# Cross-attention on one Trainium2 core: the first loads dealt between two issuing engines and turned head by head

## The chip, the cores and the metric

The kernel runs on one core of one Trainium2 chip. A core has TensorE (matmuls, into PSUM), VectorE (DVE in the profile), ScalarE (ACT), GpSimd (POOL) and SyncE (SP, which here only issues DMA transfers). Transfers are moved by 16 DMA engines. The metric is the device time of one execution in microseconds; lower is better. Everything is float32.

## The reference

Sixteen batches of 256 queries attend to 77 context rows with eight heads of 256. The output is projected, the input is added, and the sum is normalised.

```python
Q = (img_embed @ Wq).reshape(B, -1, H, D).transpose(0, 2, 1, 3)   # H = 8, D = 256
K = (sent_embed @ Wk).reshape(B, -1, H, D).transpose(0, 2, 1, 3)  # sent_embed: 16 x 77 x 192
V = (sent_embed @ Wv).reshape(B, -1, H, D).transpose(0, 2, 1, 3)
score = jnp.einsum('bhqd,bhkd->bhqk', Q, K) / math.sqrt(D)
attn = jax.nn.softmax(jnp.where(mask, score, -jnp.inf), axis=-1)
ctx = jnp.einsum('bhqk,bhkd->bqhd', attn, V).reshape(B, -1, H * D)
out = ctx @ Wo + img_embed
mu, var = jnp.mean(out, -1, keepdims=True), jnp.var(out, -1, keepdims=True)
return (out - mu) * jax.lax.rsqrt(var + EPS) * gamma + beta
```

## The kernel before

Instead of Q and K the kernel forms, for each head, G = Wk Wqᵀ / 16 (192 x 256). The product of the context with G, called a, meets the input x directly, so Q and K are never made. Wv and Wo are multiplied in the same way. G has 192 rows: the first 128 are kept in `gA` (one slice for each head), the last 64 in `gB` (two heads share one slice, one in each half of the partitions).

The order of the work is written by hand; each engine executes its instructions in the order of the program. The opening, which is all that the change touches, runs like this:

- SP issues the loads in the order of the code: `wk_nat` (Wk of heads 0, 1, first 128 rows, L623), `wq_nat` (Wq of heads 0, 1, one transfer each, L625), `wk_last` (the last 64 rows of Wk, L627), `c_sb` (the context of the first batches, L628). Then, for each pair of heads a = 1, 2, 3, four transfers of Wk and four of Wq (`load_blocks`, L598), each into 32 partitions, in blocks of 128 columns. Wv, Wo, the first input tiles, the mask and the rest of the context follow. In a `wq_blk` load a partition r takes the rows r, r + 32, r + 64 and so on of Wq.
- TensorE first runs six matmuls on zeros (`keep_busy(6)`, L664). Then it turns (transposes) the four blocks of `wk_nat` (`turn_k`), those of `wq_nat` (`turn_q`, once for each head), forms G of head 0 (`g_of`), turns `wk_last`, forms G of head 1, turns the context (`turn_c`, L714), forms the last rows of G (`rest_of_g`), and makes `a` of heads 0 and 1 (`a_of_pairs`, L181 and L193).
- For a = 1, 2, 3 the blocks are turned by DVE in squares of 32 x 32 (`turn_blk`, L703), Wk first, then Wq; TensorE makes the last 64 rows of G (`rest_of_g_of_pair`, matmul L819, tile `phb`), copied to `gB` by DVE (L828), then the first 128 (`g_of_pair`, matmul L803, tile `pgb`), copied to `gA` by ACT (L811), and then `a` of the pair.
- GpSimd makes the identity matrix for the turning, clears the unused columns of the two tiles `p_ring` (L99), and is next needed for the copy of the context's rows into `cB` (L725).

After this come the Wv and Wo products and the loop over batches (scores, softmax, product with V, normalisation), which the change leaves as it is.

Transfers and engines are joined by semaphores. The built program gives SP's transfers eight semaphores in turn; a transfer that takes a semaphore for the second time waits until the transfer that held it has landed.

Of the kernel before, what the change touches and what calls it, by code (L numbers as in the profile page):

```python
# [9 lines left out]
F32 = mybir.dt.float32  # L10
I32 = mybir.dt.int32
AF = mybir.ActivationFunctionType
ALU = mybir.AluOpType
# [3 lines left out]
P = 128  # L17
H = 8
D = 256
# [8 lines left out]
def kernel(  # L28
# [13 lines left out]
    nc = tc.nc  # L42
    B, S, DI = x.shape
    S2, DL = c.shape[1], c.shape[2]
# [6 lines left out]
    NF = H // 2  # L51
    KR = S2 - KM
    BK = 32
    NM = P // BK
# [16 lines left out]
    ps_mm = ctx.enter_context(tc.tile_pool(name="ps_mm", bufs=8, space=PSUM))  # L71
# [3 lines left out]
    ident = const.tile([P, P], F32, tag="ident", name="ident")  # L75
# [4 lines left out]
    gA = const.tile([P, H, DI], F32, tag="gA", name="gA")  # L80

    gB = const.tile([P, NF, DI], F32, tag="gB", name="gB")
# [12 lines left out]
    cRA = const.tile([P, B, KR], F32, tag="cRA", name="cRA")  # L95
    cRB = const.tile([P, B, KR], F32, tag="cRB", name="cRB")
    p_ring = [const.tile([P, NM, PW], F32, tag=f"p{i}", name=f"p_{i}") for i in range(2)]
    for p in p_ring:
        nc.gpsimd.memset(p[:, :, 2 * S2 :], 0.0)  # L99
    bias = const.tile([P, B, S2], F32, tag="bias", name="bias")  # L100
    bias_f = bias.rearrange("p b k -> p (b k)")
    bet = const.tile([P, DI], F32, tag="bet", name="bet")
# [4 lines left out]
    c_rows = c.rearrange("b k l -> (b k) l").rearrange("(r p) l -> p r l", p=CR)  # L107

    def flat(ap):
        return ap.rearrange("p a b -> p (a b)")  # L110

    def half(i):
        return slice(i * LB, (i + 1) * LB)
# [466 lines left out]
    with tc.tile_pool(name="wonce", bufs=1) as wp:  # L580
        first = -(-GB * S2 // CR)
        c_sb = wp.tile([CR, first, DL], F32, tag="c", name="c_sb")
# [3 lines left out]
        wk_nat = wp.tile([P, 2 * D], F32, tag="wk", name="wk_nat")  # L586
        wk_last = wp.tile([P, D], F32, tag="wl", name="wk_last")

        wq_blk = wp.tile([P, NF - 1, DI // BK, P], F32, tag="wqb", name="wq_blk")
        wk_blk = wp.tile([P, NF - 1, NL, P], F32, tag="wkb", name="wk_blk")  # L590
        wq_blocks = wq.rearrange("(m r) (a i f) -> a i r m f", r=BK, a=NF, i=NM)
        wk_blocks = wk.rearrange("(m r) (a i f) -> a i r m f", r=BK, a=NF, i=NM)
        wq_rows = wq[:, : 2 * D].rearrange("(t p) f -> p t f", p=P)
        wk_ends = wk[P:, : 2 * D].rearrange("r (e f) -> r e f", e=2)
# [25 lines left out]
            nc.gpsimd.tensor_copy(flat(cB)[:LB, rest], flat(cB)[LB:, rest])  # L620
            nc.gpsimd.tensor_copy(cRB, cB[:, :, KM:])

        nc.sync.dma_start(wk_nat, wk[:P, : 2 * D])  # L623
        for e in range(2):
            nc.sync.dma_start(wq_nat[:, :, e * D : (e + 1) * D], wq_rows[:, :, e * D : (e + 1) * D])  # L625
        for e in range(2):
            nc.sync.dma_start(wk_last[half(e)], wk_ends[:, e])  # L627
        nc.sync.dma_start(c_sb, c_rows[:, :first, :])  # L628
        for a in range(1, NF):
            load_blocks(wk_blk[:, a - 1], wk_blocks[a])  # L630
            load_blocks(wq_blk[:, a - 1], wq_blocks[a])
# [30 lines left out]
        def keep_busy(n):  # L662
            for i in range(n):
                nc.tensor.matmul(idle, gam[:, :P], gam[:, :P], start=True, stop=True)  # L664

        keep_busy(6)


        qT_03 = const.tile([P, 2, 4, DI], F32, tag="xg0", name="qT_03")
# [1 line left out]
        kT_03 = const.tile([P, 2, 4, DL], F32, tag="xg2", name="kT_03")  # L671
        kT_12 = const.tile([P, 2, 4, DL], F32, tag="xg3", name="kT_12")
        qT = qT_03[:, 0].rearrange("p (e dc) d -> p e dc d", e=2)
        kT = kT_03[:, 0].rearrange("p (e dc) l -> p e dc l", e=2)
# [3 lines left out]
        def turn_q(e):  # L678
            for dc, copy in enumerate((nc.vector.tensor_copy, nc.scalar.copy)):
                pt = ps_mm.tile([P, 2, P], F32, tag="mm", name=f"pt_q_{e}_{dc}")  # L680
                for t in range(2):
                    nc.tensor.transpose(
                        pt[:, t], wq_nat[:, t, e * D + dc * P : e * D + (dc + 1) * P], ident
                    )
                copy(qT[:, e, dc], flat(pt))

        def turn_k():
            pt = ps_mm.tile([P, 4, P], F32, tag="mm", name="pt_k")
            for n in range(4):
                nc.tensor.transpose(pt[:, n], wk_nat[:, n * P : (n + 1) * P], ident)  # L690
            nc.scalar.copy(kT_03[:, 0, :, :P], pt)

        def turn_k_last():
            pt = ps_mm.tile([P, 2, P], F32, tag="mm", name="pt_kl")
# [79 lines left out]
        def g_of(e):  # L774

            pg = ps_mm.tile([P, DI], F32, tag="mm", name=f"pg_{e}")
            for dc in range(2):
                nc.tensor.matmul(
                    pg, kT[:, e, dc, :P], qT[:, e, dc], start=(dc == 0), stop=(dc == 1)
                )  # L780
            nc.scalar.mul(gA[:, e], pg, D ** -0.5)

        def rest_of_g():
# [10 lines left out]
                    )  # L794
            nc.vector.tensor_scalar(gB[:, 0], ph, D ** -0.5, None, ALU.mult)

        def g_of_pair(a):

            banks = [ps_mm.tile([P, DI], F32, tag="mm", name=f"pgb_{a}_{e}") for e in range(2)]
            for n in range(4):  # L800
                for i in range(2):
                    for e in range(2):
                        nc.tensor.matmul(  # L803
                            banks[e][half(i)],
                            kT_blk[a][half(e), n, half(i)],
                            qT_blk[a][half(e), n],
                            start=(n == 0),
                            stop=(n == 3),
                        )
            for e, o in enumerate(banks):  # L810
                nc.scalar.mul(gA[:, 2 * a + e], o, D ** -0.5)  # L811

        def rest_of_g_of_pair(a):

            banks = [ps_mm.tile([P, P], F32, tag="mm", name=f"phb_{a}_{e}") for e in range(2)]
            for n in range(4):
                for i in range(2):
                    for e in range(2):
                        nc.tensor.matmul(  # L819
                            banks[e][half(i)],  # L820
                            kT_blk[a][half(e), n, P:],
                            qT_blk[a][half(e), n, i * P : (i + 1) * P],
                            start=(n == 0),
                            stop=(n == 3),
                        )
            for e, o in enumerate(banks):
                for i in range(2):
                    nc.vector.tensor_scalar(  # L828
                        gB[half(e), a, i * P : (i + 1) * P], o[half(i)], D ** -0.5, None, ALU.mult
                    )  # L830

        def a_of_pairs(*pairs, rest_first=False):
            part_A, part_B, copies = prepare_a(0, pairs, rest_first=rest_first)
# [2 lines left out]
            for dst, src in copies():  # L836
                nc.scalar.copy(dst, src)

        turn_k()
        turn_q(0)  # L840
        turn_q(1)
        g_of(0)
        turn_k_last()
        g_of(1)
# [4 lines left out]
        for a in range(1, NF):  # L849
            rest_of_g_of_pair(a)  # L850
            g_of_pair(a)
            if a < NF - 1:
                turn_blk(a + 1)
            else:
                for i in range(3):
                    turn_v(i)
            a_of_pairs(a, rest_first=True)
# [84 lines left out]
    for b in range(-1, B - 1):  # L942
# [16 lines left out]
        g, n = (b + 1) // GB + 1, (b + 1) % GB  # L959
# [126 lines left out]
```

## Time and profile before

| What | us |
|---|---|
| median of three runs (lowest to highest) | 272.66 (272.11 to 273.08) |
| the profiled execution: time | 271.64 |
| the profiled execution: span, first to last instruction | 269.8 |
| TensorE busy | 263.8 |
| DVE busy | 185.9 |
| GpSimd busy | 171.3 |
| ACT busy | 156.5 |
| first turning of Wk on TensorE starts | 4.05 |
| context, issue to landing | 4.5 |
| wq_blk loads, issue to landing (shortest, median, longest) | 4.2, 4.8, 5.0 |

Times in the profile count from the start of the span. A row of the timeline gives start, length, engine, line, operation, output and inputs, the number of instructions, and in brackets the idle time before it with what ended it. "PEld" is TensorE's loading of weights, "SPq" the queue of SP. The chain that ended last is followed back from the last instruction, at each step to what released it or to the instruction before it. A row of the windows gives the stretch and its length, busy time and number of instructions of PE, PEld, DVE, ACT and POOL, then the granted TensorE clock, the busy share of the DMA engines and GB/s.

### The profile page before, as it was taken

To read this page: it belongs to the slowest core of one execution; us is meant where nothing else is said; L and a number is where in the kernel's file an instruction comes from. 1 tells how busy PE (TensorE), PEld (TensorE's weight loads), DVE (VectorE), ACT (ScalarE), POOL (GpSimd) and SP (SyncE) were. 2 spreads that over 40 slices of the span, in tenths; PEclk is the share of its full clock that TensorE was granted. 3 is DMA by queue.
4 is the path that set the end of the run, shared out by engine and by line. 5 is a ranking of instruction groups with operands and counts; after the bars stand their busy time and mean duration, and the time that the engine had idled before them with its cause. 6 is when DMAs were issued, how large, how long until landed. Compare 5 with 4: busy or idle time off the path is not lost.

```text
span 269.8 us, 14465 instructions
## 1 busy us (share of the span) xinstructions
PE 263.8 (98%) x6152; PEld 190.7 (71%) x6152; DVE 185.9 (69%) x809; ACT 156.5 (58%) x652; POOL 171.3 (63%) x231
## 2 busy tenths in 40 slices
PE   8999999999999999999999999999999999999993
PEld 7555578854994599459954995499769969684662
DVE  1454958583564858864796379646977898988765
ACT  3244335635858555964587377728685592945752
POOL 1000005716399757995699759964999798966654
PEclk9999999999999999999999999999999999999999
DMA  6998999988000010361027100910091010110102
GB/s 196 200 198 183 305 188 154 280 147 155 5 4 4 2 45 5 97 104 41 5 62 139 44 4 15 187 41 6 5 195 46 5 43 6 41 44 2 62 22 79
DMA packets 42512, 22.69 MB, mean 84 GB/s; under 512 B 23680, under 2 KB 41680, under 8 KB 42448
## 3 DMA queue, kind: packets, MB, share of 16 engines
q1 hardware_dynamic: 42448, 21.77, 36.4%
q8 instruction: 48, 0.79, 1.2%
q14 instruction: 16, 0.13, 0.1%
HBM read 17.57 MB, written 4.19 MB: 81 GB/s over the span
## 4 chain that ended last, share of the span: by engine, by line
PE 91%; DVE 4%; DMA 3%; SPq 1%; issue 0%; DVEq 0%
PE ps L291 23%; PE pa L181 12%; PE pv L215 11%; PE po L436 10%; PE pm L436 9%; PE pa L193 6%; PE pv L226 6%; PE po L369 4%; PE pu L742 3%; PE pgb L803 2%; DMA wq_blk<-in_L_xattn_Wq_dram 2%; DMA c_sb<-in_ctx_dram 2%; PE pr L251 1%; PE pw L756 1%; PE phb L819 1%; PE pr L262 1%
## 5 line engine op out<-in xcount | busy, mean ns | idle before, releaser
L326 ACT ACTIVATE e<-s,top 128x77 f32<-128x77 f32 x256 | 83.8, 346 | 45.5 <-DVE top L308 38.5
L291 PE MATMUL ps<-a,xT 128*32 128x154 f32 x2048 | 69.9, 294 | 0.0
L291 PEld LDWEIGHTS ps<-a,xT 128*32 128x32 f32 x2048 | 66.2, 110 | 1.2 <-issue 0.4
L347 POOL TENSOR_TENSOR p<-e,rden 128x512 f32<-128x512 f32 x64 | 47.7, 771 | 23.3 <-DVE rden L341 23.3
L308 DVE CUSTOM_DVE_ANT_0 s<-ps,bias 128x77 f32<-128x77 f32 x256 | 43.6, 232 | 15.4 <-PE ps L291 15.3
L326 ACT ACTIVATION_READ_ACCUMULATOR e<-s,top 128x1 f32 x208 | 39.0, 187 | 0.0
L181 PE MATMUL pa<-cA,gA 128*32 128x308 f32 (+1 forms) x576 | 36.6, 394 | 0.0
L471 POOL TENSOR_TENSOR xg<-xg,m 128x256 f32<-128x256 f32 x39 | 28.7, 737 | 7.8 <-DVE xg L485 5.8
L181 PEld LDWEIGHTS pa<-cA,gA 128*32 128x32 f32 x576 | 18.3, 110 | 21.1 <-issue 6.7
L215 PE MATMUL pv<-uA,cA 128*32 128x512 f32 x256 | 30.6, 595 | 0.0
L554 DVE SCALAR_TENSOR_TENSOR xg<-xg,rstd,bet 128x256 f32<-128x256 f32 x26 | 21.2, 816 | 12.9 <-ACT rstd L515 11.5
L400 POOL TENSOR_TENSOR ts<-vw 128x768 f32<-128x768 f32 x13 | 24.0, 1847 | 7.6 <-ACT vw L928 7.6
L357 DVE STREAM_TRANSPOSE pT<-p 128x640 f32<-128x640 f32 x32 | 25.7, 822 | 3.2 <-POOL p L347 3.1
L928 ACT COPY vw<-pv 128x512 f32<-128x512 f32 x32 | 17.7, 584 | 14.7 <-PE pv L215 7.7
L485 DVE TENSOR_TENSOR xg<-po,xg 128x256 f32<-128x256 f32 x31 | 11.6, 407 | 13.4 <-PE po L436 12.4
L308 DVE DVE_READ_ACCUMULATOR2_ANT top<- 128x1 f32 x256 | 20.8, 81 | 0.0
L574 POOL TENSOR_TENSOR nan<-nan 128x4 f32<-128x4 f32 (+1 forms) x2 | 0.4, 209 | 31.8 <-DVE nan L573 31.8
L193 PE MATMUL pa<-cB,gB 64*32 64x308 f32 (+1 forms) x576 | 20.6, 392 | 0.0
L928 ACT COPY a<-pa 128x308 f32<-128x308 f32 (+1 forms) x56 | 18.9, 399 | 1.7 <-PE pa L181 0.2
L193 PEld LDWEIGHTS pa<-cB,gB 64*32 64x32 f32 x576 | 10.6, 106 | 12.2 <-issue 7.7
L226 PE MATMUL pv<-uB,cB 64*32 64x512 f32 x256 | 17.3, 597 | 0.0
L535 DVE SCALAR_TENSOR_TENSOR xg<-xg,mv,gam 128x256 f32<-128x256 f32 x27 | 16.7, 619 | 0.1
(119 smaller groups left out, 412.1 us busy)
## 6 DMA issues: line engine op xcount, KB each, us to landing
xT<-in_x_dram SPq DMA_DIRECT2D x32, 128.0 KB, 5.9
xg<-in_x_dram SPq DMA_DIRECT2D x6, 512.0 KB, 5.2
out_dram<-xg SPq DMA_DIRECT2D x11, 256.0 KB, 2.3
wo<-in_L_xattn_Wo_dram SPq DMA_DIRECT2D x4, 512.0 KB, 5.3
wq_blk<-in_L_xattn_Wq_dram SPq DMA_DIRECT2D x12, 128.0 KB, 4.8
wvT<-in_L_xattn_Wv_dram SPq DMA_DIRECT2D x16, 96.0 KB, 3.6
out_dram<-xg SPq DMA_DIRECT2D x10, 128.0 KB, 1.7
wk_blk<-in_L_xattn_Wk_dram SPq DMA_DIRECT2D x12, 96.0 KB, 4.5
```

Of the source, the lines that this page charges most:

```text
L181: nc.tensor.matmul(flat(o[i * BK : (i + 1) * BK]), gA[:, h, cols(dc, i)], flat(cA[:, batches, :]), start=not rest_first and n in opening, ...
L193: nc.tensor.matmul(flat(banks[j + k][i * BK : (i + 1) * BK]), gB[half(k), h // 2, cols(dc, i)], flat(cB[half(k), batches, :]), start=rest_ ...
L215: nc.tensor.matmul(pv[k][i * BK : (i + 1) * BK], cA[:, b, k * BK : (k + 1) * BK], uA[:, parts, :, i], start=not rest_first, stop=rest_first,)
L226: nc.tensor.matmul(pv[k][i * BK : (i + 1) * BK], cB[half(k), b, k * BK : (k + 1) * BK], uB[half(k), parts, :, i], start=rest_first, stop=n ...
L291: nc.tensor.matmul(ps[m // 2][i * BK : (i + 1) * BK, m % 2 * 2 * S2 : (m % 2 + 1) * 2 * S2], xT_of[g][:, j * NM + m, dc], flat(a_of[g][:, ...
L308: nc.vector.tensor_tensor_reduce(s[:, h], ps[a][:, k * S2 : (k + 1) * S2], bias[:, b, :], scale=-1.0, scalar=FAR, op0=ALU.add, op1=ALU.min ...
L326: nc.scalar.activation(e[:, h], s[:, h], AF.Exp, bias=top[:, one], scale=-1.0, accum_out=den[:, one] if t < QT * NS else None,)
L347: nc.gpsimd.tensor_tensor(part, e_mh[:, :, :, keys], rden_mh.unsqueeze(3).to_broadcast(list(part.shape)), ALU.mult,)
L357: nc.vector.transpose(pT_of[t].rearrange("p n m q -> p m n q"), p.rearrange("p m (n k) -> p m n k", k=BK),)
L436: nc.tensor.matmul(out[i * BK : (i + 1) * BK], weight[:, i], moving, start=first and n == 0, stop=final and n == len(terms) - 1,)
L471: nc.gpsimd.tensor_tensor(to, to, what, ALU.add)
L928: nc.scalar.copy(dst, src)
```

## The change

Five edits belong together.

- The first 128 rows of Wk come in two transfers, one for each head, and alternate with those of Wq; `turn_k` is split in the same way, so that TensorE turns Wk and Wq of head 0, then those of head 1. ACT copies each half by itself.
- The two transfers of `wk_last` and that of `c_sb` are issued by GpSimd instead of SP, ahead of the clearing of `p_ring`, which moves behind them.
- `keep_busy` runs five matmuls instead of six.
- Wq of heads 2 and 3 (a = 1 alone) is loaded with the rows dealt differently: partition r takes the eight neighbouring rows 8r to 8r + 7.
- That puts the columns of G of these heads in another order. The copies from PSUM to `gA` (ACT) and `gB` (DVE) read with a step of 32 elements and put the columns back in place.

```diff
-    for p in p_ring:
-        nc.gpsimd.memset(p[:, :, 2 * S2 :], 0.0)
...
-        wq_blocks = wq.rearrange("(m r) (a i f) -> a i r m f", r=BK, a=NF, i=NM)
+        by_rows, dealt = ("(m r)", "(r m)")
+        wq_blocks = [
+            wq.rearrange(f"{dealt if a == 1 else by_rows} (a i f) -> a i r m f", r=BK, a=NF, i=NM)[a]
+            for a in range(NF)
+        ]
...
-        nc.sync.dma_start(wk_nat, wk[:P, : 2 * D])
         for e in range(2):
+            nc.sync.dma_start(wk_nat[:, e * D : (e + 1) * D], wk[:P, e * D : (e + 1) * D])
             nc.sync.dma_start(wq_nat[:, :, e * D : (e + 1) * D], wq_rows[:, :, e * D : (e + 1) * D])
         for e in range(2):
-            nc.sync.dma_start(wk_last[half(e)], wk_ends[:, e])
-        nc.sync.dma_start(c_sb, c_rows[:, :first, :])
+            nc.gpsimd.dma_start(wk_last[half(e)], wk_ends[:, e])
+        nc.gpsimd.dma_start(c_sb, c_rows[:, :first, :])
+        for p in p_ring:
+            nc.gpsimd.memset(p[:, :, 2 * S2 :], 0.0)
...
-        keep_busy(6)
+        keep_busy(5)
...
-        def turn_k():
-            pt = ps_mm.tile([P, 4, P], F32, tag="mm", name="pt_k")
-            for n in range(4):
-                nc.tensor.transpose(pt[:, n], wk_nat[:, n * P : (n + 1) * P], ident)
-            nc.scalar.copy(kT_03[:, 0, :, :P], pt)
+        def turn_k(e):
+            pt = ps_mm.tile([P, 2, P], F32, tag="mm", name=f"pt_k_{e}")
+            for dc in range(2):
+                nc.tensor.transpose(
+                    pt[:, dc], wk_nat[:, e * D + dc * P : e * D + (dc + 1) * P], ident
+                )
+            nc.scalar.copy(kT[:, e, :, :P], pt)
...
+        def dealt_rows(ap):
+            return ap.rearrange("p (r m) -> p r m", r=BK)
...
-                nc.scalar.mul(gA[:, 2 * a + e], o, D ** -0.5)
+                to = gA[:, 2 * a + e]
+                if a == 1:
+                    to, o = dealt_rows(to), o.rearrange("p (m r) -> p r m", r=BK)
+                nc.scalar.mul(to, o, D ** -0.5)
...
-                    nc.vector.tensor_scalar(
-                        gB[half(e), a, i * P : (i + 1) * P], o[half(i)], D ** -0.5, None, ALU.mult
-                    )
+                    to, of = gB[half(e), a, i * P : (i + 1) * P], o[half(i)]
+                    if a == 1:
+                        to = dealt_rows(gB[half(e), a])[:, :, i * NM : (i + 1) * NM]
+                        of = of.rearrange("p (m r) -> p r m", r=BK)
+                    nc.vector.tensor_scalar(to, of, D ** -0.5, None, ALU.mult)
...
-        turn_k()
-        turn_q(0)
-        turn_q(1)
+        for e in range(2):
+            turn_k(e)
+            turn_q(e)
```

## The prediction

> **What bounds the kernel now.** I read the busy times, the chain that ended last, the chain and the timeline of the first 18 us, and the windows of DMA traffic, in this order.
>
> ```profile
> PE 263.8 (98%) x6152; PEld 190.7 (71%) x6152; DVE 185.9 (69%) x809; ACT 156.5 (58%) x652; POOL 171.3 (63%) x231
> ...
> PE 91%; DVE 4%; DMA 3%; SPq 1%; issue 0%; DVEq 0%
> ```
>
> TensorE is busy for 263.8 of 269.8 us and holds 91% of the chain; DMA holds 3%. The change touches only loads and copies ahead of 18 us, so it can only move the moment from which TensorE runs without a gap. The chain says what sets that moment (start, length, what; us):
>
> ```profile
> 2.14 0.56 SPq L627
> ...
> 2.74 0.59 SPq L627
> ...
> 3.37 4.53 DMA c_sb<-in_ctx_dram
> 7.90 0.02 issue
> 7.92 4.60 DMA wq_blk<-in_L_xattn_Wq_dram
> ...
> 12.64 1.26 DVE qT L703
> 13.90 0.04 issue
> 13.95 1.10 PE phb L819 x32
> ```
>
> Two landings stand in series: the last of the four wq_blk loads of heads 2, 3 is issued at 7.92 because the context landed at 7.90. The built program gives SP's transfers eight semaphores in turn, so each waits until the one eight places before it has landed; the context is that one. Then the block is turned, and TensorE starts phb at 13.95. The timeline shows how much of this TensorE feels (start, length; idle before it in brackets):
>
> ```profile
> 1.05 2.93 PE L664 MATMUL idle<-gam 128*128 128x128 f32 x12 [1.05 <-DVE eps L78]
> ...
> 4.05 1.09 PE L690 MATMUL pt_k<-ident,wk_nat 128*128 128x128 f32 x4
> ...
> 4.93 1.79 PE L682 MATMUL pt_q<-ident,wq_nat 128*128 128x128 f32 x8
> ...
> 6.57 1.03 PE L778 MATMUL pg<-qT,kT 128*128 128x256 f32 x4
> ...
> 8.52 0.74 PE L714 MATMUL pc<-ident,c_sb 112*128 112x112 f32 x6
> ...
> 13.95 1.10 PE L819 MATMUL phb<-qT,kT 64*64 64x128 f32 x32 [0.27 <-DVE qT L703]
> ```
>
> Only 0.27 us of idle time: from 4.05 to 13.68 TensorE had other work. So the wait by itself is worth 0.27, and more only if that work, 9.63 us, starts earlier too. The windows tell how full the DMA engines are (last number GB/s):
>
> ```profile
> 2.00:5.00 3.00, 2.93 (x15) 2.66 (x14) 0.00 (x0) 0.02 (x1) 0.00 (x0) 1.00 0.90 295
> 5.00:6.00 1.00, 1.00 (x6) 1.00 (x5) 0.40 (x1) 0.59 (x1) 0.00 (x0) 1.00 0.85 243
> 6.00:8.00 2.00, 2.00 (x12) 1.82 (x12) 0.61 (x3) 1.12 (x3) 0.00 (x0) 1.00 1.02 195
> 8.00:12.00 4.00, 4.00 (x46) 2.34 (x48) 2.17 (x5) 0.90 (x4) 0.59 (x2) 1.00 1.22 199
> ```
>
> The first weights, in pieces of 1 or 2 KB, move at 295 GB/s; the blocks, in pieces of 512 B, at 199, with the engines full.
>
> **The change part by part.**
>
> *Head by head.* One of six idle matmuls goes (2.93/6 by its spacing of 0.43), so TensorE is free at 3.6 instead of 4.05. wk_nat (256 KB) landed at 0.73 + 3.2 = 3.9; its half saves 128 KB at 295 GB/s, 0.44, and lands at 3.5. By the same count Wq of head 0 (before: 4.6) comes at 4.2, Wk of head 1 at 4.6, Wq of head 1 unchanged at 5.5, since the same bytes stand ahead of it. Turning takes 0.43 for two blocks of Wk, 0.85 for four of Wq. So: Wk 3.6 to 4.03; wait; Wq 4.2 to 5.05; Wk 5.05 to 5.48; Wq 5.55 to 6.40. pg starts at 6.40 instead of 6.57, and phb could start at 13.68 − 0.17 = 13.51: 0.44 under 13.95. Without any wait for data it would be 3.6 + 9.63 = 13.23 (−0.72). The extra ScalarE copy (one of 0.59 becomes two of 0.37) lies in ScalarE's idle time, 3.16 us before it; should that cover go, it costs 0.15.
>
> *GpSimd issues three transfers.* SP loses 0.56 + 0.59 + 0.59 and gains one issue of 0.38: its blocks are issued 1.4 us earlier, at 2.55, and the last wq_blk at 2.55 + 7 × 0.48 = 5.9, now waiting only for Wq of head 1 at 5.5. Behind that wait stand SP's blocks of heads 4 to 7, which DVE turns with over 1 us to spare before 20.11. An earlier issue helps only where the engines ran thin: at 5 to 6 us (243 against 295 GB/s, 52 KB, which is 0.26 at 199 GB/s). So wq_blk lands between 12.26 (that alone) and 10.5 (the whole 2.0), phb is ready between 13.69 and 11.9. Taken: 12.1, ready at 13.5, level with TensorE.
>
> GpSimd issues nothing in this trace. Low bound of an issue: SP's rows for the same transfers, 0.58; high: the longest issue of a block on SP, 1.44. GpSimd is free at 1.30 (identity done). With the context's issue to landing of 4.53, it lands at 7.0 (low), 7.8 (1.0 each, taken, nearer the like transfers) or 8.7 (high). TensorE wants it at 8.3 now, 8.1 then. wk_last, first in the queue, is wanted at 7.2 and lands by 2.74 + 3.6 = 6.3 even at the high end. The two memsets behind them are for columns first needed after 52 us; GpSimd's next work, the copy at 10.02, leaves over 4 us.
>
> These transfers no longer stand behind Wq of head 1 but beside it. Bounds: nothing of them moves ahead (0), or all 380 KB (1.32 at 295 GB/s). Taken: 0 to 64 KB, 0.1; the first cannot land before 1.30 + 3.2 = 4.5, and part of it fills the thin stretch after 5 us.
>
> A rule speaks against this part: the Trainium skill, "DMA: Bandwidth & Descriptors", section "Issuing engines are not separate DMA queues", says that transfers from all issuing engines share the same sixteen DMA engines and that a second issuer saves only issue time. By it alone the gain would be the issue time that was not covered; the windows agree, with engines at 1.02 to 1.22 after 6 us and 0.85 only at 5 to 6 us. The page "SBUF — State Buffer", section "SBUF: two separate sides", adds that GpSimd cannot write a transfer's descriptors while VectorE holds their shared port; here VectorE runs nothing between 1.01 and 5.61, so by that rule too the price would be nothing.
>
> *Dealt rows.* The load's pieces stay 512 B. Bounds for its 512 KB: 295 GB/s, as the first weights (1.78 us instead of 2.63, −0.85), or 142 GB/s, the slowest window of small pieces (42 to 44 us: 3.69, +1.06). Taken: no change, since piece size is what tells the rows apart. The copies of G now read PSUM at steps of 32 elements. Nearest row for a step: the transpose of Wv, which picks every fourth element, against that of Wk with runs of 32, both 768 elements:
>
> ```profile
> L731 DVE STREAM_TRANSPOSE wv_turned<-wvT 128x768 f32<-128x768 f32 x4 | 6.2, 1614 | 0.0
> ...
> L703 DVE STREAM_TRANSPOSE kT<-wk_blk 128x768 f32<-128x768 f32 x2 | 1.9, 974 | 0.0
> ```
>
> By 1.66, VectorE's four copies (15.10, 0.29 each) end 0.77 later, at 17.1, and pa, which starts at 16.70, waits 0.4; ScalarE's two (0.38 each, from 16.82) then end at 18.1, ahead of the matmuls L181 that read gA (17.90 + 0.4). Below nothing is excluded, as the count of elements stays. Taken 0.05, nearer the plain copies.
>
> *Sum.* −0.44 + 0.1 + 0.05 = −0.3 in the profiled execution: span 269.8 becomes 269.5, time 271.64 becomes 271.35. The median shown, 272.66, is 1.02 above that execution. The chain's DMA share stems from the two landings in series (4.53 + 4.60 of 269.8); I put half of the 1.02, an estimate, on late landings, which one landing instead of two lets through less. Against the median: −0.3 − 0.5 = −0.8, **271.8 us**. About 0.3%, 0.8 us, is what this measurement can tell from no change.
>
> **Rivals.** Numbers 2 to 4 are set on the median, without the half of the spread.
> 1. *Landings explain all the spread*: −0.3 − 1.0, 271.4; the no-wait bound of −0.72 supports it. Against: series and spread are not tied by any view.
> 2. *GpSimd's bytes go ahead of Wq of head 1.* All 380 KB give +1.32 − 0.44 = +0.9, 273.5; 200 KB give +0.25, 272.9. For: they start at 1.30. Against: their landing takes 3.2 or more.
> 3. *The other side: GpSimd issues late*, and TensorE, in order, stands at pc. It decides from 1.2 us an issue (landing 8.2). At 1.44, 0.6 late: −0.3 + 0.6 = +0.3; at 2.0 each, 9.8, 1.7 late: +1.4, 274.0. For: no such row exists; against: SP needs 0.58.
> 4. *Dealt rows cost*: the slow read (landing 13.2, ready 14.5, +0.6, 273.3), or the slow copies (0.4 eats the gain, 272.7).
>
> **How the numbers follow.** Forecast 0.48 (faster 0.29, same 0.19; its own range 271.2 to 272.4), rival 1 0.12 (faster), rival 2 0.12 (same 0.06, slower 0.06), rival 3 0.19 (slower 0.17, same 0.02), rival 4 0.09 (slower 0.06, same 0.03). Together faster 0.41, same 0.30, slower 0.29. The range of 270.9 to 273.7 leaves out the far ends of rivals 1 and 3.
>
> **What would show it.** Right: first pt_k near 3.6, pg near 6.4 to 6.5, no gap before pc, phb at 13.4 to 13.7, the chain's DMA share smaller and without c_sb. Wrong: idle time of TensorE before pt_q or pc that ends with wq_nat, wk_last or c_sb; issues on GpSimd over 1.2 us; a landing of wq_blk after 12.5; copies of gB over 0.45 us. Any change in the stage after 50 us would contradict the whole reading.

## The result, and the profile after

The changed kernel takes 274.93 us (median of 22 runs, 272.36 to 276.78); the kernel before, run beside it, 272.1 (22 runs). The ratio is 1.0083, 95% interval 1.0061 to 1.0105: about 0.8% slower. It compares the means without four slow runs (one of 347.68 of the kernel before, and 276.49, 276.57 and 276.78 of the changed one); the medians of all runs give 1.0104. The forecast was 271.8 and a range up to 273.7, so both the sign and the range are missed. The profiled execution is one of the quicker ones: 272.60 with a span of 270.8, against 271.64 and 269.8 before.

The waits of TensorE in the first 18 us of the changed kernel (engine, line, what it waited for: us in total, times, longest):

```profile
PE pt_q L686 <- DMA wq_nat<-in_L_xattn_Wq_dram: 1.4, 2, 1.1
...
PE pt_k L694 <- DMA wk_nat<-in_L_xattn_Wk_dram: 0.5, 1, 0.5
```

Before the change the only data that TensorE waited for in this stretch was qT, 0.3 us. The chain of the first 18 us names the new bound (start, length, what):

```profile
2.15 4.98 DMA wq_nat<-in_L_xattn_Wq_dram
7.13 0.04 issue
7.18 0.66 PE pt_q L686 x4
7.83 0.86 PE pg L784 x4
```

One transfer, the second half of `wq_nat` (Wq of head 1), takes 4.98 us from its issue and lands at 7.13. Before, it was issued at 1.63 and landed at 5.49. From then on TensorE is never short of work, as the timeline shows (start, length; idle before it in brackets):

```profile
3.35 0.66 PE L694 MATMUL pt_k<-ident,wk_nat 128*128 128x128 f32 x2
4.26 0.84 PE L686 MATMUL pt_q<-ident,wq_nat 128*128 128x128 f32 x4 [0.25 <-DMA wq_nat<-in_L_xattn_Wq_dram]
5.59 0.44 PE L694 MATMUL pt_k<-ident,wk_nat 128*128 128x128 f32 x2 [0.49 <-DMA wk_nat<-in_L_xattn_Wk_dram]
7.18 0.66 PE L686 MATMUL pt_q<-ident,wq_nat 128*128 128x128 f32 x4 [1.14 <-DMA wq_nat<-in_L_xattn_Wq_dram]
...
9.62 0.74 PE L720 MATMUL pc<-ident,c_sb 112*128 112x112 f32 x6
...
14.71 1.10 PE L831 MATMUL phb<-qT,kT 64*64 64x128 f32 x32
```

The first turning starts 0.7 us sooner than before (3.35 against 4.05) and `phb` 0.76 later (14.71 against 13.95). `phb` has lost its wait for `wq_blk`, as was meant, because everything ahead of it is late.

Who took the DMA engines is in the view of the transfers. A row gives queue, packets, MB, and share of the 16 engines' time; q1 is SP's queue, q0 GpSimd's. First the stretch from 3.5 us to the start of the last packet of Wq of head 1 (5.8), then 5.5 to 7.1 us, the end of the wait:

```profile
q1 hardware_dynamic: 510, 0.42, 60.9%
q0 software_dynamic: 71, 0.18, 25.9%
```

```profile
q0 software_dynamic: 67, 0.22, 65.3%
q1 hardware_dynamic: 227, 0.12, 39.4%
```

While Wq of head 1 is under way, GpSimd's queue moves 0.18 MB beside it. At the end of the wait GpSimd's queue has two thirds of the engines, but this stretch says little about Wq: in the trace's packet records only 20 of q1's 227 packets there have the 1024 bytes in which Wk and Wq of heads 0, 1 come, the last of them starts at 5.79, and 190 have the 512 bytes of SP's next blocks. From that last packet to the landing pass 1.3 us. From 3.5 to 7.5 us q0 moved 0.38 of 0.95 MB. In the same four microseconds of the kernel before, all 0.98 MB were q1's.

The median lies 2.3 us above this profiled execution, which the experiments have to explain too.

### The profile page after: what moved, and what is told of

Its sections match the earlier page's. It is cut to its first block, busy times and chain, and to the rows that moved or that the text cites. A ratio compares the mean times of both kernels' runs of the same rounds, so it can differ in the third digit from the quotient of the medians.

```text
span 270.8 us, 14469 instructions
## 1 busy us (share of the span) xinstructions
PE 263.0 (97%) x6150; PEld 189.3 (70%) x6150; DVE 185.4 (68%) x809; ACT 156.8 (58%) x653; POOL 173.4 (64%) x234
## 4 chain that ended last, share of the span: by engine, by line
PE 93%; DVE 3%; DMA 2%; SPq 0%; issue 0%; DVEq 0%
PE ps L289 23%; PE pa L179 12%; PE pv L213 10%; PE po L434 10%; PE pm L434 8%; PE pa L191 6%; PE pv L224 6%; PE po L367 4%; PE pu L748 3%; PE pgb L812 2%; DMA wq_nat<-in_L_xattn_Wq_dram 2%; PE pr L249 1%; PE pw L762 1%; PE phb L831 1%; PE pr L260 1%; DVE s L306 1%
```

## The experiments

All ratios are against the kernel before, run on the same chip in the same batch. The table gives, from each profile, the landing of Wq of head 1, the first lasting grant of TensorE's full clock (from the trace's clock records), the starts of `pc` and `phb`, and the span; then the ratio of the runs. "Idle" is `keep_busy`'s work.

```
kernel                                  Wq h1  grant    pc    phb   span   ratio (95%)
before                                   5.49   6.47   8.52  13.95  269.8  1
after                                    7.13   4.69   9.62  14.71  270.8  1.0083 (1.0061-1.0105)
y4 after, profiled again                 8.29  11.76  12.44  17.53  273.6  1.0096 (1.0069-1.0124)
x2 after, SP issues all                  5.38   5.61   8.23  13.74  271.0  1.0006 (0.9979-1.0032)
x3 before + GpSimd issues                7.84   6.40  10.33  15.42  272.3  1.0101 (1.0070-1.0132)
x4 after, no dealt rows                  6.73  10.38  10.96  16.05  272.1  1.0129 (1.0086-1.0173)
x1 after + some idle matmuls             7.33   4.13   9.82  14.91  271.5  1.0074 (1.0045-1.0103)
y1 before, 1 idle matmul                 5.51   8.28   9.42  14.51  270.4  1.0021 (1.0007-1.0035)
y2 after, ScalarE issues                 8.54  11.65  12.51  17.60  274.2  1.0155 (1.0133-1.0176)
y3 after, GpSimd issues wk_last only     7.58  13.04  12.37  17.79  273.8  1.0103 (1.0055-1.0150)
z1 before + head by head alone           5.81   5.78   8.68  14.15  270.4  1.0008 (0.9992-1.0023)
z2 z1 + context by GpSimd, held back     5.45   4.10   8.77  13.86  269.8  0.9987 (0.9972-1.0001)
z3 after + more idle matmuls             6.75   5.52   9.52  14.61  271.3  1.0069 (1.0042-1.0096)
z4 x2 + 16 KB by GpSimd                  5.75   4.77   8.26  13.86  270.0  1.0011 (0.9990-1.0032)
u1 z2 + G of head 1 before wk_last       5.80   5.51   8.45  13.55  269.5  0.9960 (0.9945-0.9974)
u2 after, GpSimd's issues held back      6.32  10.13  10.63  15.72  271.8  1.0041 (1.0025-1.0057)
u3 z2, not held back                     7.86  10.74  11.72  16.81  272.8  1.0099 (1.0076-1.0121)
```

### Undoing and isolating the parts

**x2_sp_issues**: the changed kernel with the three transfers back on SP.

```diff
-            nc.gpsimd.dma_start(wk_last[half(e)], wk_ends[:, e])
-        nc.gpsimd.dma_start(c_sb, c_rows[:, :first, :])
+            nc.sync.dma_start(wk_last[half(e)], wk_ends[:, e])
+        nc.sync.dma_start(c_sb, c_rows[:, :first, :])
```

> The changed kernel with the three transfers of wk_last and the context issued by SP again, after Wq of head 1. Theory (GpSimd's 380 KB run beside SP's queue and push Wq of head 1 from 5.5 to 7.1 us): Wq of head 1 lands at 5.4 to 5.6, no wait of TensorE over 0.3 us in the opening, ratio 0.996 to 1.000 to the kernel before. Rival (the dealt rows, in the reading or in the strided copies, are what costs): still slower, ratio 1.004 to 1.008.

Measured 271.99 us. Its timeline of TensorE:

```profile
5.47 0.67 PE L686 MATMUL pt_q<-ident,wq_nat 128*128 128x128 f32 x4
...
13.74 1.10 PE L831 MATMUL phb<-qT,kT 64*64 64x128 f32 x32 [0.33 <-DVE qT L709]
```

Wq of head 1 lands at 5.38, and the ratio, 1.0006, is just above the theory's range and far below the rival's. With the issuer put back, the wait for Wq of head 1 is gone, the old wait for qT is back, and so is the time. `phb` is 0.21 earlier than before, but the span is 1.2 longer: in this execution the rest of the context landed at 45.82 instead of 44.46, and TensorE paused 0.36 at 47.2 for rows made from it, and 0.57 more at 49.9 behind VectorE, from where the chain leads back to the same landing. So a second stage of this kernel is tied to landings as well, and one profile of it is worth no more than such a landing.

**x3_gpsimd_alone**: the kernel before with only the issues moved to GpSimd (the same four lines the other way, and the clearing of `p_ring` behind them).

> The kernel before with one part of the change: GpSimd issues wk_last and the context. Six idle matmuls, Wk in one transfer, rows as before. Theory: Wq of head 1 lands at 6.3 to 7.1 instead of 5.5, TensorE waits 0.5 to 1.2 us for it, ratio 1.002 to 1.008, with a granted clock that may dip as in the changed kernel. Rival (head by head or the dealt rows cost): ratio 0.997 to 1.001.

Measured 274.83 us; Wq of head 1 lands at 7.84 and TensorE waits 1.85 us before its second `pt_q`. All three, with the ratio of 1.0101, lie beyond the theory's ranges, so the cause was right and its size too small. This one edit, put into the kernel before, costs what the whole change costs, and taken out of the changed kernel it leaves 1.0006.

**x4_by_rows**: the changed kernel without dealt rows (`by_rows` for all heads, plain copies of G).

> The changed kernel without the dealt rows: Wq of heads 2, 3 is read by rows r, r + 32 and so on again, and the copies of G are plain. Theory: no difference to the changed kernel beyond 0.5 us, ratio 1.006 to 1.011 to the kernel before, since Wq of heads 2, 3 is not waited for. Rival (dealing costs): back to 0.997 to 1.002. A third way (dealing helps a late load): ratio 1.011 or more.

Measured 275.93 us (6 runs). Dealing is not the cause; without it the kernel is no faster. The ratio of 1.0129 lies in the range of the third way (dealing helps), but its interval reaches down to 1.0086 and overlaps that of the changed kernel, so a help isn't shown either. The last `wq_blk` lands at 12.37 here and at 12.42 with dealing, and the copies settle the rest. The costliest groups of the changed kernel (last numbers before the second bar: busy us, mean ns of one):

```profile
L844 DVE TENSOR_SCALAR gB<-phb 64x128 f32<-64x128 f32 x12 | 3.5, 289 | 7.9 <-PE phb L831 7.6
...
L823 ACT ACTIVATE gA<-pgb 128x256 f32<-128x256 f32 x6 | 2.0, 382 | 6.5 <-PE pgb L812 6.5
```

and the same groups of the kernel before:

```profile
L828 DVE TENSOR_SCALAR gB<-phb 64x128 f32<-64x128 f32 x12 | 3.5, 289 | 6.6 <-PE phb L819 6.3
...
L811 ACT ACTIVATE gA<-pgb 128x256 f32<-128x256 f32 x6 | 2.0, 381 | 6.9 <-PE pgb L803 6.9
```

Four of the twelve and two of the six read PSUM at a step of 32 elements, and the means are the same. One by one, too: the four with a step take 283 to 295 ns, the same four of the kernel before 282 to 295. What dealing does cost is issue time: the four `wq_blk` issues of heads 2, 3 took SP 0.56 to 0.69 us each, and 0.31 to 0.46 in x4. Here the wait for Wq of head 1 covered it.

**z1_heads_alone**: the kernel before with the loads and the turning head by head, five idle matmuls, and nothing else.

> The kernel before with the head by head loads and turning alone: SP issues everything, five idle matmuls, plain rows. Theory (the second queue is what delays the second head's Wq): it lands at 5.4 to 5.6 as before, TensorE waits under 0.3 before its last pt_q, phb starts at 13.4 to 13.8, ratio 0.997 to 1.000. Rival (turning head by head makes TensorE pause and its clock come late by itself): a grant after 7 or a withdrawal, phb at 14.3 or later, ratio 1.002 to 1.005.

Measured 272.24 us. Both miss: the rival's late clock doesn't show (grant at 5.78), but neither does a gain, and Wq of head 1 is 0.2 past its range: the last `wq_blk` is still issued at 8.56, when the context has landed at 8.54, and `phb` waits 0.28 for it. The two landings in series are still there, and turning head by head alone gives nothing that can be measured.

### What about the second issuer costs

**y2_act_issues**: ScalarE issues the three transfers instead of GpSimd (`nc.scalar.dma_start`).

> The changed kernel with wk_last and the context issued by ScalarE, behind the load of its table, instead of GpSimd. Theory A (any second queue takes its share of the sixteen engines, byte for byte): Wq of head 1 lands at 6.3 to 7.1 as in the changed kernel, ratio 1.005 to 1.011. Theory B (GpSimd's queue takes more than its share: its pieces run in packets of 4096 and 4608 B against packets of 512 and 1024 B on SP's queue, turn by turn): Wq of head 1 lands at 5.6 to 6.2, ratio 0.998 to 1.004.

Measured 276.07 us (5 runs), the slowest of all; Wq of head 1 lands at 8.54. That is beyond theory A's ranges, and theory B's are far off. Its packets are of 768 and 1024 bytes, where GpSimd's are of 4096, 4608 and 2304; so neither GpSimd's way of issuing nor its large packets are needed for the loss. ScalarE's issues also start at 0.76, and GpSimd's at 1.48, so its bytes compete for longer.

**y3_wk_last_only**: the changed kernel with the context back on SP; GpSimd issues `wk_last`, 128 KB, alone.

> The changed kernel with the context issued by SP again, and only the 128 KB of wk_last by GpSimd. Theory (bytes on GpSimd's queue go ahead of Wq of head 1): it lands at 5.4 + 0.43 = 5.8, up to 6.0, between 5.4 with none and 7.1 with all 380 KB; ratio 0.999 to 1.005. Rival (the use of GpSimd's queue costs by itself, whatever it carries): 6.7 to 7.1, ratio 1.006 to 1.010.

Measured 275.57 us (6 runs); Wq of head 1 lands at 7.58. The theory, with 5.8 to 6.0, falls. A third of the bytes does as much harm: 128 KB at 240 GB/s would be 0.55 us, so the loss is not simply the bytes at the usual rate. The windows show one more part. First a kernel without a second queue (x2), then this one (stretch and length, busy time and number of PE, PEld, DVE, ACT, POOL, then granted clock, DMA share, GB/s):

```profile
3.50:4.50 1.00, 0.84 (x5) 0.45 (x4) 0.00 (x0) 0.37 (x1) 0.00 (x0) 1.00 0.94 315
```

```profile
3.50:4.50 1.00, 0.96 (x5) 0.56 (x5) 0.00 (x0) 0.37 (x1) 0.00 (x0) 1.00 0.62 191
```

In the microsecond in which GpSimd's first packets run, the engines together move 191 instead of 315 GB/s; in the changed kernel itself it is 202. The 124 KB that were not moved are another 0.4 us at 300 GB/s. But a kernel with one queue has such a slow microsecond too, one later, when `wk_last` and the first of the context run behind Wq. In x2:

```profile
4.50:5.50 1.00, 1.00 (x7) 0.85 (x6) 0.42 (x1) 0.21 (x1) 0.00 (x0) 1.00 0.89 183
```

In the kernel before it is 212. Over both microseconds together x2 moves 249 GB/s and y3 253. So it isn't shown that two queues move less than one: the slow microsecond may belong to these transfers, and on the second queue it falls ahead of the last packets of Wq. More than half of the 2.2 between 5.38 (x2) and 7.58 stays open. The engines also finish unevenly: of the sixteen parts of Wq of head 1 the first and last completed at 4.36 and 5.49 before, and at 5.27 and 7.13 after, while packets of the next transfers (512 bytes, `wk_blk`) were already moving. The size of this share was not measured by itself.

**z4_small**: x2 and one transfer of 16 KB by GpSimd at the same moment.

```diff
+        small = const.tile([P, 32], F32, tag="small", name="small")
+        nc.gpsimd.dma_start(small, wk[:P, :32])
```

> The changed kernel with its three transfers back on SP, and a transfer of 16 KB, which nobody reads, issued by GpSimd at about 1.5. Theory 'bytes' (what the second queue moves ahead of the second head's Wq delays it): Wq of head 1 lands at 5.4 to 5.7, phb at 13.6 to 13.9, ratio 0.999 to 1.003. Rival 'the use of a second queue by itself': Wq lands at 6.3 or later and its sixteen parts end over 1.5 us apart, ratio 1.005 to 1.011.

Measured 272.11 us; Wq of head 1 lands at 5.75. The mere use of the second queue, as a cost by itself, falls: with 16 KB no change of the time can be measured, while `wk_last`'s 128 KB cost 1%. The two runs differ in what follows Wq on SP's queue as well, so the size alone isn't tested.

**u3_context_early**: `z2` (below) without its hold: GpSimd issues only the context, at 1.57.

> The kernel with the late context without the copy that holds it back: GpSimd issues the context's 252 KB at about 1.45 and nothing else. Theory (the moment is what counts): the context's packets share the engines with the second head's Wq, which lands at 6.5 to 8; phb at 14.3 or later, ratio 1.005 to 1.012. Rival (the context on GpSimd is harmless, wk_last alone did it): Wq lands under 6, phb under 14, ratio 0.997 to 1.002.

Measured 275.01 us (6 runs). The timeline of TensorE:

```profile
7.90 1.11 PE L682 MATMUL pt_q<-ident,wq_nat 128*128 128x128 f32 x4 [2.10 <-DMA wq_nat<-in_L_xattn_Wq_dram]
8.81 1.91 PE L780 MATMUL pg<-qT,kT 128*128 128x256 f32 x4
```

The context, issued at 1.57, lands at 6.66, 1.2 us ahead of Wq of head 1, which TensorE needs first. So either transfer does the harm alone. Everything else, the order on SP's queue included, is as in z2, which costs nothing: here the early second queue by itself is the cause.

### The clock

The second line of the timeline of u3 holds another cost. Its four matmuls of `pg` last 1.91 us here and 1.03 in the changed kernel's profile.

**y4_after_again**: the changed kernel once more, unchanged, to see an execution nearer its median.

> The changed kernel as it is, beside the others on one chip. Theory: ratio 1.006 to 1.011, Wq of head 1 at 6.7 to 7.4, and in some executions the step to full clock at about 10 us, as without the dealt rows. If the dealt rows made the load of heads 2, 3 better, it would be clear of the kernel without them (1.0129, from 1.0086 to 1.0173) on the low side.

Measured 275.15 us (10 runs), the profiled one 275.39. Timeline, then a window:

```profile
8.33 1.12 PE L686 MATMUL pt_q<-ident,wq_nat 128*128 128x128 f32 x4 [2.27 <-DMA wq_nat<-in_L_xattn_Wq_dram]
9.24 1.92 PE L784 MATMUL pg<-qT,kT 128*128 128x256 f32 x4
...
12.44 0.74 PE L720 MATMUL pc<-ident,c_sb 112*128 112x112 f32 x6
```

```profile
8.00:12.00 4.00, 3.67 (x12) 3.11 (x13) 0.81 (x2) 0.76 (x2) 0.00 (x0) 0.57 1.23 195
```

The window's granted clock is 0.57: full clock was granted at 4.93, taken back from 8.35 to 11.76 after the pause, and granted again. Against the first profile, `phb` is 2.82 later (17.53 to 14.71). Of this, 1.15 is the later start of the last `pt_q` (8.33 to 7.18) and 1.67 the way from there to `pc` (4.11 instead of 2.44), at half speed; from `pc` to `phb` both take 5.09. So this execution near the median is a longer wait, and then a slow clock behind it. Wq of head 1 landed at 8.29, past the 7.4 that was expected. Its mean clock is 0.989; 7 of the 22 runs of the changed kernel have 0.985 to 0.990. In other kernels the first grant itself came late (10.38 in x4, 13.04 in y3); there the windows print 1.00, since no record lies before the first grant, and only the length of the matmuls tells. So a mean clock near 1 doesn't rule out a late first grant.

**y1_no_idle**: the kernel before with `keep_busy(1)` instead of `keep_busy(6)`.

> The kernel before with one idle matmul in the opening instead of six; transfers, landings and all other work as before, so that TensorE pauses from about 1.7 to 4.0 us and nothing that it waits for comes later. Theory (part of the loss is the clock: TensorE runs at half speed until it has been busy for long enough, and pauses put that off): the opening's transposes run at 0.21 us each for longer than 6.4 us, the step to 0.11 comes at 8 to 11 us, phb starts 0.3 to 2 us later, ratio 1.001 to 1.008. Rival (the clock plays no part, the loss is all in the late landing): no change, ratio 0.998 to 1.001.

Measured 272.71 us. The landings stay (Wq of head 1 at 5.51). TensorE idles for 2.2 us before 4.08, when it has nothing to do anyway, and that idleness costs:

```profile
4.08 1.08 PE L690 MATMUL pt_k<-ident,wk_nat 128*128 128x128 f32 x4 [2.23 <-DMA wk_nat<-in_L_xattn_Wk_dram]
...
6.67 1.83 PE L778 MATMUL pg<-qT,kT 128*128 128x256 f32 x4
```

The grant comes at 8.28 instead of 6.47, and `phb` 0.56 later, as the theory said. This is the clock by itself, with no landing of the opening moved by more than 0.14.

**x1_filled**: the changed kernel with one idle matmul before the second `turn_k` and three before the second `turn_q`.

> The changed kernel with four more idle matmuls: one before Wk of head 1 is turned, three before Wq of head 1. They lie in TensorE's waits (0.49 and 1.14 us in the profile after); loads and data are as they were. Theory (the waits cost twice: by themselves, and because TensorE's clock is granted later or withdrawn when it pauses in the opening; in the 22 runs the mean granted clock was 0.985 to 1.0, and the profiled run had 1.0): the mean clock of every run is 0.999 or more, the spread shrinks to about 1 us, and the time falls to 272.6 to 273.4, ratio 1.002 to 1.005. Rival (the runs that are slower than the profiled one have later landings): no change, 274 to 275.5, ratio 1.006 to 1.011, spread 4 us.

Measured 273.94 us. The ratio of 1.0074 lies in the rival's range (the landing alone costs), and the mean clock went down to 0.994, not 0.999. Two waits of 0.66 and 0.50 were left unfilled, so it settles little.

**z3_filled_more**: idle matmuls in all waits (1, 2 and 5).

```diff
+            keep_busy((0, 2)[e])
             turn_k(e)
+            keep_busy((1, 5)[e])
             turn_q(e)
```

> The changed kernel with idle matmuls in all three waits (1 before Wq of head 0, 2 before Wk of head 1, 5 before Wq of head 1), so that TensorE does not pause before 7. Wq of head 1 lands at 7.0 to 7.8 as in the changed kernel. Theory (landing and clock both cost; the clock costs in those executions where the grant is late or withdrawn): grant at 4 to 5 in every execution, mean clock never below 0.994, pg at 0.9 to 1.1 us, phb at 14.3 to 14.9, ratio 1.003 to 1.007, with a narrower spread than the changed kernel run beside it earlier (1.010). Rival (the clock has no share, the landing is all): ratio 1.008 to 1.011.

Measured 273.87 us (6 runs, 272.95 to 274.7; the changed kernel reached 276.8). Wq of head 1 lands at 6.75, TensorE hardly pauses, `pg` takes 1.03 and no execution has a mean clock under 0.995, where 7 of the 22 of the changed kernel have 0.985 to 0.990. In these six runs the high end is gone, the shift of about 1.9 us stays. So the landing looks like the larger part, with the clock widening it; the early grant (5.52) is seen in the profiled execution alone. How much of the median is the clock's can't be read off, because the intervals (1.0042 to 1.0096, and 1.0061 to 1.0105) overlap.

### The same transfers, later

**z2_context_late**: z1, with the context issued by GpSimd after a tiny copy that must wait for the first Wk.

```diff
-        nc.sync.dma_start(c_sb, c_rows[:, :first, :])
+        late = const.tile([P, 1], F32, tag="late", name="late")
+        nc.gpsimd.tensor_copy(late, wk_nat[:, :1])
+        nc.gpsimd.dma_start(c_sb, c_rows[:, :first, :])
```

> Head by head, with the context alone on GpSimd, held back by a GpSimd copy that reads the first Wk (landed at 3.2 to 3.3), so that it is issued at about 3.6 to 4.4 and its packets come behind most of the second head's Wq. Theory (a second queue costs only while the second head's Wq is under way): Wq of head 1 lands at 5.4 to 5.9, the context at 7.8 to 8.4, the last wq_blk is issued at about 6 without waiting for the context and lands at 12.0 to 12.5, phb at 13.3 to 13.7, ratio 0.995 to 1.000. Rival (a second queue costs whenever it runs beside the first): the blocks become uneven too and land after 12.8, or Wq lands after 6.5; phb at 14.3 or later, ratio 1.004 to 1.012.

Measured 271.62 us. The context is issued at 3.36 instead of 1.57 (u3), Wq of head 1 lands at 5.45 instead of 7.86, and the ratio falls from 1.0099 to 0.9987 (0.9972 to 1.0001). From 3.0 to 5.05 us only SP's queue moves:

```profile
q1 hardware_dynamic: 618, 0.57, 92.7%
```

The last `wq_blk`, whose issue now waits for `wk_last` (7.52) and no longer for the context, lands at 11.55, earlier than the theory's 12.0 and a full microsecond before the 12.52 of the kernel before. It isn't yet in `phb` (13.86, where 13.7 was the theory's latest), because TensorE waits elsewhere:

```profile
7.65 0.41 PE L700 MATMUL pt_kl<-ident,wk_last 128*128 128x128 f32 x2 [0.64 <-DMA wk_last<-in_L_xattn_Wk_dram]
```

**u1_late_swap**: the same with `g_of(1)` ahead of `turn_k_last()`.

> The kernel with the late context, with G of head 1 formed before the last rows of Wk are turned, so that TensorE has 0.87 of work in the 0.64 that it waited for wk_last. Theory (that wait is what still holds phb at 13.86, since wq_blk lands at 11.6): phb at 13.3 to 13.5, ratio 0.995 to 0.998. Rival (TensorE waits for the context in its place, which landed at 8.3): a wait before pc of 0.2 to 0.5, phb at 13.6 to 13.9, ratio 0.998 to 1.000.

Measured 271.3 us (271.14 to 271.58, 5 runs), ratio 0.996, interval 0.9945 to 0.9974: it beats both the changed kernel and the one before. The interval of z2 (0.9972 to 1.0001) still touches this one, so the swap's own share is not clear of noise. Its timeline:

```profile
5.85 0.66 PE L684 MATMUL pt_q<-ident,wq_nat 128*128 128x128 f32 x4 [0.19 <-DMA wq_nat<-in_L_xattn_Wq_dram]
6.34 1.89 PE L782 MATMUL pg<-qT,kT 128*128 128x256 f32 x8
8.21 0.41 PE L700 MATMUL pt_kl<-ident,wk_last 128*128 128x128 f32 x2
8.45 0.74 PE L718 MATMUL pc<-ident,c_sb 112*128 112x112 f32 x6
...
13.55 1.10 PE L823 MATMUL phb<-qT,kT 64*64 64x128 f32 x32
```

No bracket after 5.85: TensorE has work without a gap, and the rival's wait before `pc` is not there. `phb` is 0.05 past the theory's range; Wq of head 1 landed at 5.80 here and at 5.45 in z2.

**u2_all_late**: the changed kernel with its three GpSimd transfers behind the same copy.

> The changed kernel, whole, with its three GpSimd transfers held back by one small GpSimd copy that reads the first half of Wk (landed at 3.2). Theory (what costs is that GpSimd's queue runs beside the second head's Wq; later the same bytes and the same queue cost little): Wq of head 1 lands at 5.4 to 6.0, no pause of TensorE over 0.6 before the last pt_q, the clock granted by 6.5 and kept, phb at 13.7 to 14.4, no execution over 274.5, ratio 0.999 to 1.004. Rival (GpSimd's issuing costs whenever it is used): Wq lands after 6.5 or the blocks after 13, phb at 14.7 or later, ratio 1.006 to 1.012.

Measured 273.46 us: between the two. Wq of head 1 lands at 6.32, not 7.1 to 8.3, and the ratio falls from 1.0083 to 1.0041. The theory's direction holds, but it misses its numbers: some by little (Wq by 0.3, the ratio by 0.0001, one execution of 274.7), and those of the clock and of `phb` by much, where the rival's hold:

```profile
6.37 1.12 PE L688 MATMUL pt_q<-ident,wq_nat 128*128 128x128 f32 x4 [0.76 <-DMA wq_nat<-in_L_xattn_Wq_dram]
7.27 1.92 PE L786 MATMUL pg<-qT,kT 128*128 128x256 f32 x4
```

The pause of 0.76 was followed by a grant at 10.13, and `phb` at 15.72. It wasn't GpSimd's bytes that made Wq late here. From 3.5 to 5.3 us its queue moves nothing:

```profile
q1 hardware_dynamic: 595, 0.45, 83.2%
```

The last packet of Wq starts at 5.36. SP's blocks, which stand right behind Wq of head 1 here, were moving from 4.5 on while its last parts were still owed. So SP's own next transfers are the likely reason that Wq lands 0.5 to 0.9 later than in z1 (5.81) and x2 (5.38). The changed kernel, x3 and x4 have the same order on SP's queue, so a part of their loss may be this; no run takes it alone.

## Why the prediction was wrong

*The step that failed: "Taken: 0 to 64 KB, 0.1".* For GpSimd's transfers beside Wq of head 1 the text had bounds of 0 and 1.32 (all 380 KB) and chose near the lower end. Measured: Wq of head 1 landed 1.64 later than before (7.13 to 5.49) in the profile, and 2.8 later in y4. Pricing by bytes was the fault, not only the number of bytes. When the last packet of Wq started, q0 had moved 0.18 MB in the profile and 0.36 MB in y4; at the rates of those stretches (261 and 230 GB/s) that is 0.7 and 1.6 us, and the delays are about 1 us longer. With 128 KB alone (y3) the delay was 2.1. How the rest divides among the slow microsecond (y3), SP's own blocks (u2) and the uneven end was not measured. The outcome is the second rival's, which was given 0.12. Its +0.9 fits the profiled execution (+0.96), but not the median (+2.8), and its upper bound of 1.32 was too low: y3 and y4 are beyond it.

The reason for 0.1 was that the first GpSimd transfer "cannot land before 4.5". It landed at 5.36, but its packets ran from 3.7 on. A late landing does not keep its packets, and those of the next transfers, from running before: the landing is the last of them. And the rows that were read to price the shift were about *whether* the engines were full. What it left out is *whose* packets a full engine takes. It also counted the earlier issue of SP's blocks as a gain alone; u2 gives reason to think that it has a price.

*The rule cited for it.* The Trainium skill, "DMA: Bandwidth & Descriptors", section "Issuing engines are not separate DMA queues", says that a second issuer saves only issue time. It held: from 3.5 to 7.5 the changed kernel moved 237 GB/s in all, the kernel before 244. The same page's section "Queues, rings and completion order" was the one to weigh: an engine serves the queues that have work in turn, packet by packet. Within one queue, says the section, an engine takes descriptors in order; between two it does not. The profile agrees: 0.18 MB of q0 ran from 3.5 to 5.8 beside what was left of Wq of head 1, although Wq was issued at 2.15, before the second half of `wk_last` (2.22) and the context (2.74).

*GpSimd's issues.* Three were priced at 1.0 each, bounds 0.58 to 1.44; they took 0.73, 0.53 and 0.72, as the timeline of GpSimd shows:

```profile
1.48 1.26 POOL L629 DMA_DIRECT2D wk_last<-in_L_xattn_Wk_dram  x2 [0.17 <-issue]
2.74 0.72 POOL L630 DMA_DIRECT2D c_sb<-in_ctx_dram  x1
```

The third rival (issues over 1.2 us) falls. The context landed at 8.64, later than the 7.8 taken, though issued earlier: 5.9 us from its issue, not 4.53. TensorE did not wait for it, being late itself. The second half of `wk_last` landed at 6.91, and the text had 6.3 at the latest.

*Head by head.* The first `pt_k` came at 3.35 (forecast 3.6), Wq of head 0 at 4.22 (4.2). Wk of head 1, forecast for 4.6, landed at 5.55 beside GpSimd's packets and at 4.54 in x2: the working was right without the second queue. The −0.44 at `phb` became −0.21 in x2, and +0.20 in z1, with ratios of 1.0006 and 1.0008: no gain that can be measured by itself.

*SP's blocks earlier.* The last `wq_blk` was to land at 12.1 and landed at 12.42 (12.52 before): it was issued at 7.15 behind the late Wq, not at 5.9. In z2 and u1, where Wq of head 1 is nearly on time and `wk_last` stays between it and the blocks, it landed at 11.55 and 11.31, within the text's bounds of 10.5 to 12.26.

*Dealt rows.* Taken at 0.05, measured 0: same copy times, same landing (12.42, and 12.37 in x4). The fourth rival falls.

*The clock was not in the text*, a term put at nothing without a reason. The text priced the pause of TensorE as the time of the pause alone. y1 shows 0.56 for idleness with no other change, y4 1.67 for a clock taken back. The Trainium skill, "TensorE: Matmul & The Clock Gate", Part 1, says that full clock needs a busy window of about 3.4 us, that an idle window takes it back, and that the windows run freely, so that the moment varies from run to run. The records of y4 agree in the length: 3.41 us granted, 3.41 withdrawn. They don't agree that a whole idle window is needed: the pause ahead of the withdrawal was 2.27. The grants in the table, of kernels with different pauses, lie anywhere from 4.1 to 13.0.

*Half of the spread.* The text put 0.5 of the 1.02 between the median of three runs and the profiled run on landings and took it off the forecast. In the later batches, with 17 to 29 runs each, the kernel before had medians of 271.9 to 272.2, 0.3 to 0.6 above that execution; so about half of the 1.02 was chance in three runs. The best version gains 0.9 in the median and 0.3 in the span of its profile.

*After 50 us.* Said to contradict the whole reading if it changed. Of the 1.0 of span, 0.76 arises by `phb`, and it is still 0.76 at the first `po` (75.00 and 74.24); the remaining 0.2 comes later, and no run explains it. x2 shows a tie that the reading had overlooked: a late landing of the rest of the context costs TensorE time at 47 to 50 us.

## What to carry to other kernels

Moving a transfer to a second issuing engine takes it out of the order of the first queue: it then runs beside the load that is needed next, and here that cost more than its bytes. So check what is needed first, and what moves up behind it in the first queue. If the second issuer is worth having, hold its transfers back with a small dependence until the urgent load is nearly in, and then look for the next wait: here the context held back gave 0.9987 instead of 1.0099, and with one swap behind it 0.996. A pause of TensorE in the opening can cost more than its length when its clock has yet to be granted or can be taken back: leaving out five idle matmuls, in a stretch without other work, cost 0.56 us at `phb` (y1).

## What the runs showed of the hardware that was not expected

- In the microsecond in which GpSimd's first packets ran, both queues together moved 191 and 202 GB/s (y3, the changed kernel), against 315 in x2 and 290 with only 16 KB on the second queue (z4). With one queue the slow microsecond came one later (183 in x2, 212 before).
- A transfer's last packet is not its landing: in the changed kernel the last packet of Wq of head 1 started at 5.79, and it landed at 7.13.
- A pause of 2.27 us was enough for TensorE's full clock to be withdrawn for 3.41 us (y4), and one of 0.76 stood before a grant as late as 10.13 (u2). Pauses of 1.14 (the changed kernel's profile) and 1.85 (x3) were not followed by a withdrawal in their executions.
- Reading PSUM at a step of 32 float32 elements cost VectorE and ScalarE nothing: 283 to 295 ns for 64 x 128 and 378 to 384 for 128 x 256, and 282 to 295 and 377 to 384 without a step.
